# One attention and top-1-expert kernel: expert tables read five halves after their loads, one transposed tile to a half, late expert tiles from half 13 on

## The chip, the cores and the metric

The kernel runs on one NeuronCore of one Trainium2 chip. The metric is the device time of one execution in microseconds (us). Five engines work from instruction streams of their own: TensorE (PE in the profile, with its weight loads as PEld), VectorE (DVE), ScalarE (ACT), GpSimd (POOL) and SyncE (SP), which here only issues transfers. POOL also issues transfers, among them all that add while they copy and all that are indexed.

## The reference, cut to what matters

```python
xn = layernorm(x)                                  # x: 4 batches x 2048 tokens x 512
# attention, 16 heads of 32; q and k go through rfft * sigmoid(mask) * irfft
q, k, v = split(xn @ w_qkv)
attn = softmax(filter(q) @ filter(k).T / sqrt(32))
a = (attn @ v) @ w_out + b_out
# top-1 experts, 8 of them, the first 100 tokens of each, one shared weight matrix
probs = softmax(xn @ w_gate);  best = argmax(probs);  gate = max(probs)
location = cumsum(one_hot(best)) - 1               # over all tokens, in order
kept = location < 100                              # at most 800 tokens in all
f[token] = gate * (xn[token] @ w_expert + b_expert)  if kept else 0
out = x + a + f
```

All arithmetic is in float32.

## The kernel before, in words

**Rounds, blocks and halves.** A round k handles one batch and one group of four heads; there are 16 rounds (k = 4 * batch + group). A round has four blocks of 512 queries, and a block runs over 16 tiles of 128 keys. The work for one key tile is called a half, so that a round has 64 halves (`GH`), a block 16 (`HB`), and the whole kernel 1024. Two halves make a window. In each half PE does four matmuls of queries of a later block against keys, whose row maxima DVE takes, four score matmuls, ACT takes two exponentials, and PE multiplies the tile of the half before with the values (four matmuls into one bank, called the products here), which DVE adds to `num`.

**The side work.** All else is done beside this: projections of the next round, one 128-token piece to a step (16 small matmuls and a copy by ACT); the closing steps of the block before (`fold`, eight `invert`, `divide`, four `result`, then `add`, which adds a 1 MB chunk `y` to the output by a POOL transfer); the transposing of the next batch's normalized tokens (`turn`, four transposes and a copy); the routing of tokens to experts; and the experts themselves. `at(half, step)` appends a step to the agenda of a half, and `behind` puts it after all others of that half. `level` then spreads the projection pieces over the halves by a release, a latest half, and the costs that the other steps have declared.

**The denominators.** After each window POOL issues a 1 MB transfer that adds the tile `odd` into the tile `even` (`pair`, in the next window), and a window later adds the running sum to it with two instructions of its own (`add_to`). There are three buffers for `odd` and five for `even`. An exponential into `odd` therefore waits for the landing of the pair transfer of three windows before.

**The experts.** Routing writes each kept token's number and gate into one of four DRAM tables by indexed transfers. In round 12, the first of the last batch, `place_experts` lays out what follows: `begin` loads the expert weights, the bias and the four tables, reduces the tables on DVE (`entry`, `who`) and clears the first token buffer; `clear_rest` clears the second; `fetch` gathers seven tiles of tokens; `measure` takes their statistics on DVE; `scale` makes their factors on POOL (four small instructions); `expert(i)` normalizes tile i on ACT, transposes tile i-1 and multiplies tile i-2, for the first four tiles. Three late tiles are transposed and multiplied in the last round, as `LATE` says: one half for `turn_row`, four for `expert_columns`. Each tile's result is then added to the output rows in three POOL steps, two halves apart: `gather_row` (indexed read of the output), `add_row`, `scatter_row` (indexed write).

**Order.** `InOrder` keeps every instruction of an engine in program order, so an instruction that waits holds all behind it on its engine. All these instructions are recorded through one helper, and the profile has them at line 83; they are told apart by their tiles.

Of the kernel before, what the change touches and what calls it, by code (L numbers as in the profile page):

```python
# [12 lines left out]
F32 = mybir.dt.float32  # L13
# [20 lines left out]
SLOTS = E * CAP  # L34
ST = -(-SLOTS // P)
EARLY = 4
LATE = ((14, 15, 16, 22, 23), (24, 25, 26, 27, 28), (29, 30, 31, 32, 38))
NTAB = 4
FAR = 1 << 20
EPS = 1e-5  # L40
# [62 lines left out]
def attention_and_top1_experts(ctx: ExitStack, tc: tile.TileContext, a: dict, out: bass.AP):  # L103
# [457 lines left out]
    def expert_steps():  # L561


        def begin():
            w_exp = chunk("w_exp")
            on.sync.dma_start(out=w_exp, in_=a["L0_ffn_w_expert"].rearrange("(r p) n -> p r n", p=P))
            b_exp = work.tile([P, DM], F32, tag="b_exp", name="b_exp", bufs=1)
            on.sync.dma_start(out=b_exp, in_=a["L0_ffn_b_expert"].partition_broadcast(P))
            entries = small.tile([P, NTAB, ST, 2], F32, name="entries")
            for i, table in enumerate(tables):  # L570
                on.sync.dma_start(out=entries[:, i], in_=table.rearrange("(t p) c -> p t c", p=P))
            entry = small.tile([P, ST, 2], F32, name="entry1")
            for i, op in enumerate((ALU.min, ALU.max)):
                on.vector.tensor_reduce(
                    entry[:, :, i], entries[:, :, :, i].rearrange("p n t -> p t n"), AX.X, op
                )
            who = small.tile([P, ST], I32, name="who")
            on.vector.tensor_copy(who, entry[:, :, 0])
            xg = [chunk("xg"), small.tile([P, ST - TQ, DM], F32, name="xg1")]
            on.gpsimd.memset(xg[0], 0.0)  # L580
            mv = small.tile([P, ST, 2], F32, name="mv1")
            index = [bass.IndirectOffsetOnAxis(ap=who[:, i : i + 1], axis=0) for i in range(ST)]
            bound = {"bounds_check": B * S - 1, "oob_is_err": False}
            taken.update(mv=mv, w_exp=w_exp, b_exp=b_exp, entry=entry, index=index, bound=bound, xg=xg)

        def clear_rest():
            on.gpsimd.memset(taken["xg"][1], 0.0)

        def row(i):
            return taken["xg"][i // TQ][:, i % TQ, :]  # L590

        def fetch(i):
            on.gpsimd.indirect_dma_start(row(i), None, rows, taken["index"][i], **taken["bound"])

        def measure(i):
            stats = small.tile([P, 6], F32, name="stats1")
# [12 lines left out]
        def turn_row(i):  # L609
            px = bank()  # L610
            for r in range(NR):
                on.tensor.transpose(px[:, r * P : (r + 1) * P], row(i)[:, r * P : (r + 1) * P], ident)
            taken["xt"] = work.tile([P, QB], F32, tag="byx", name="xt", bufs=1)
            on.scalar.copy(taken["xt"], px)

        def expert_columns(i, q):
            cols = slice(q * P, (q + 1) * P)
            pe = bank()[:, cols]
            for r in range(NR):
                columns(  # L620
                    pe,
                    taken["xt"][:, r * P : (r + 1) * P],
                    taken["w_exp"][:, r, cols],
                    start=(r == 0),
                    stop=(r == NR - 1),
                )
            on.vector.tensor_tensor(row(i)[:, cols], pe, taken["b_exp"][:, cols], ALU.add)
            if q == NR - 1:
                on.scalar.activation(row(i), row(i), AF.Copy, scale=taken["entry"][:, i : i + 1, 1])

        def expert(i):

            if 2 <= i < EARLY + 2:
                at = slice(i - 2, i - 1)
                pe = bank()
                for r in range(NR):
                    on.tensor.matmul(
                        pe,
                        lhsT=taken["xt"][:, r * P : (r + 1) * P],
                        rhs=taken["w_exp"][:, r, :],  # L640
                        start=(r == 0),
                        stop=(r == NR - 1),
                    )
# [11 lines left out]
        return clear_rest, begin, fetch, measure, scale, expert, turn_row, expert_columns  # L655

    def gather_row(i):
        if i < EARLY:
# [366 lines left out]
    def place_experts(start):  # L1025


        clear_rest, begin, fetch, measure, scale, expert, turn_row, expert_columns = expert_steps()
        first = start + 36
        at(first, begin)  # L1030
        at(first + 5, clear_rest)
        for i in range(ST):
            at(first + 2 + 2 * i, fetch, i)
            at(start + (46, 47, 48, 53, 55, 56, 57)[i], measure, i)
        at(first + 22, scale)
        for i in range(ST):
            at(first + 26 + 2 * i, expert, i, cost=(NR if 2 <= i < EARLY + 2 else 0) + (1 if 1 <= i <= EARLY else 0))
        tail = start + 3 * GH
        for i, (turned, *places) in enumerate(LATE):
            at(tail + turned, turn_row, EARLY + i, cost=0.5)  # L1040
            for q, half in enumerate(places):
                at(tail + half, expert_columns, EARLY + i, q, cost=1)
        for i in range(ST):
            free = start + GH + i * HB + 26 if i < EARLY else tail + (25, 30, 39)[i - EARLY]
            for step in (gather_row, add_row, scatter_row):
                at(free, step, i)
                free += 2
# [64 lines left out]
        for n in range(NQ):  # L1112
            at(start + GH - 10 + n * TQ, key_steps, n)

    TURNS = (2, 4, 6, 6, 6, 7, 7, 8, 12, 12, 12, 13, 16, 19, 21, 22)
    SPENT = GH - HB - MAX_AHEAD // 2 + TQ
    ROUTE = len(first_route)
    assert ROUTE == 12 + NT + 1
# [174 lines left out]
```

## Time and profile before

| what | value |
|---|---|
| median of 3 runs | 4135.46 us (4131.81 to 4139.23) |
| the profiled execution | 4130.4 us, of which the span is 4128.6 us |
| granted TensorE clock | 0.999 of full speed |
| PE busy | 4105.5 us (99% of the span) |
| DVE busy | 3418.3 us (83%) |
| POOL busy | 3015.6 us (73%) |
| ACT busy | 2486.1 us (60%) |
| POOL's transfer queue | 601.63 MB, 74.7% of 16 engines' span |

The page gives busy time for each engine, the span in 40 slices, the transfer queues, and the chain of work that ended last. The timeline lists instructions with start, duration and, in square brackets, the idle time of the engine ahead of it and what ended that. Since a half has one group of products (PE `odd,v` or `even,v`), the distance from the start of one such group to the next is the length of a half, and what PE does in between says which side work it held.

### The profile page before, as it was taken

To read this page: it belongs to the slowest core of one execution; us is meant where nothing else is said; L and a number is where in the kernel's file an instruction comes from. 1 tells how busy PE (TensorE), PEld (TensorE's weight loads), DVE (VectorE), ACT (ScalarE), POOL (GpSimd) and SP (SyncE) were. 2 spreads that over 40 slices of the span, in tenths; PEclk is the share of its full clock that TensorE was granted. 3 is DMA by queue.
4 is the path that set the end of the run, shared out by engine and by line. 5 is a ranking of instruction groups with operands and counts; after the bars stand their busy time and mean duration, and the time that the engine had idled before them with its cause. 6 is when DMAs were issued, how large, how long until landed. Compare 5 with 4: busy or idle time off the path is not lost.

```text
span 4128.6 us, 122052 instructions
## 1 busy us (share of the span) xinstructions
PE 4105.5 (99%) x53184; PEld 1832.0 (44%) x53184; DVE 3418.3 (83%) x4876; ACT 2486.1 (60%) x3424; POOL 3015.6 (73%) x2122
## 2 busy tenths in 40 slices
PE   9999999999999999999999999999999999999999
PEld 5444445444444444444444444444444444444442
DVE  7888887978888888797888888888788888888885
ACT  4555565676655556567665556566666555665665
POOL 1678776776887777676787766767678777786787
PEclk9999999999999999999999999999999999999999
DMA  4787887987788878899788788789887887877877
GB/s 127 147 165 154 160 165 160 226 186 147 154 161 162 163 155 161 188 203 193 145 158 160 158 161 160 159 191 208 171 160 151 173 163 150 170 163 156 163 152 147
DMA packets 179488, 680.81 MB, mean 165 GB/s; under 512 B 23478, under 2 KB 54360, under 8 KB 114184
## 3 DMA queue, kind: packets, MB, share of 16 engines
q0 software_dynamic: 109856, 601.63, 74.7%
q1 hardware_dynamic: 69024, 71.34, 5.3%
q8 instruction: 416, 6.82, 0.6%
q14 instruction: 120, 0.98, 0.1%
q10 hardware_dynamic: 72, 0.03, 0.0%
HBM read 71.07 MB, written 87.91 MB: 39 GB/s over the span
## 4 chain that ended last, share of the span: by engine, by line
PE 97%; DVE 1%; DMA 1%; POOL 0%; issue 0%; ACT 0%; SPq 0%; POOLq 0%; ACTq 0%; DVEq 0%
PE array L83 97%; DVE part L83 1%; POOL even L83 0%; DMA even<-odd 0%; DMA entries<-table 0%; DMA odd<-in_L_attn_w_qkv_dram 0%; ACT xs L83 0%; DVE num L83 0%; ACT xnT L83 0%; DVE factor L83 0%; DMA table<-entry,slot 0%; DVE stats L83 0%; POOL out_dram L83 0%; ACT odd L83 0%; POOL rest L83 0%
## 5 line engine op out<-in xcount | busy, mean ns | idle before, releaser
L83 DVE TENSOR_REDUCE part<-array 128x1 f32<-128x512 f32 (+1 forms) x3066 | 2480.7, 865 | 630.4 <-PE array L83 625.4
L83 POOL TENSOR_TENSOR even<-even 128x1024 f32<-128x1024 f32 x876 | 2123.9, 2527 | 466.7 <-DMA even<-odd 465.8
L83 PE MATMUL array<-keys,q 32*128 32x512 f32 x8192 | 2040.9, 613 | 2.5 <-ACT keys L83 0.8
L83 PE MATMUL array<-q,steps_of_keys 32*128 32x512 f32 x8128 | 2009.7, 614 | 0.2
L83 ACT ACTIVATE odd<-array 128x1024 f32<-128x1024 f32 x1024 | 994.7, 1021 | 462.5 <-PE array L83 388.0
L83 ACT ACTIVATE even<-array 128x1024 f32<-128x1024 f32 x1014 | 983.7, 1021 | 417.8 <-PE array L83 409.5
L83 PEld LDWEIGHTS array<-keys,q 32*128 32x128 f32 x8192 | 760.1, 184 | 540.7 <-DVE part L83 326.7
L83 PEld LDWEIGHTS array<-q,steps_of_keys 32*128 32x128 f32 x8128 | 690.4, 183 | 243.4 <-issue 227.0
L83 DVE TENSOR_TENSOR num<-num,array 128x512 f32<-128x512 f32 x960 | 651.0, 678 | 37.7 <-PE array L83 37.7
L83 POOL DMA_DIRECT2D even<-odd x504 | 462.4, 917 | 277.1 <-ACT odd L83 235.6
L83 PEld LDWEIGHTS array<-xnT,w 128*32 128x32 f32 x16384 | 460.0, 110 | 286.3 <-DVE part L83 196.0
L83 PE MATMUL array<-odd,v 128*32 128x512 f32 x4096 | 546.3, 605 | 0.5 <-DVE part L83 0.5
L83 PE MATMUL array<-even,v 128*32 128x512 f32 x4056 | 540.1, 605 | 3.3 <-DVE part L83 3.3
L83 PE MATMUL array<-xnT,w 128*32 128x128 f32 x16384 | 534.7, 273 | 1.1 <-ACT xnT L83 1.0
L83 PEld LDWEIGHTS array<-w,xnT 128*32 128x32 f32 x8192 | 231.5, 110 | 144.6 <-DVE part L83 100.3
L83 DVE RECIPROCAL factor<-den 128x64 f32<-128x64 f32 x504 | 274.7, 546 | 0.0
L83 PE MATMUL array<-w,xnT 128*32 128x128 f32 x8192 | 267.9, 273 | 0.1
L83 PE MATMUL array<-wo,ot 128*32 128x512 f32 x2048 | 266.7, 593 | 0.0
L83 PEld LDWEIGHTS array<-odd,v 128*32 128x32 f32 x4096 | 80.7, 108 | 388.6 <-DVE part L83 380.6
L83 PEld LDWEIGHTS array<-even,v 128*32 128x32 f32 x4056 | 79.8, 108 | 387.9 <-DVE part L83 383.4
L83 POOL DMA_DIRECT2D out_dram<-y x63 | 87.4, 1387 | 156.3 <-ACT y L83 112.1
L83 ACT COPY keys<-array 128x128 f32<-128x128 f32 x256 | 68.2, 266 | 176.8 <-PE array L83 172.3
(152 smaller groups left out, 1540.5 us busy)
## 6 DMA issues: line engine op xcount, KB each, us to landing
even<-odd POOLq DMA_DIRECT2D x504, 1024.0 KB, 8.3
out_dram<-y POOLq DMA_DIRECT2D x63, 1024.0 KB, 9.9
xs<-in_L_attn_x_dram SPq DMA_DIRECT2D x96, 256.0 KB
out_dram<-in_L_attn_x_dram SPq DMA_DIRECT2D x16, 1024.0 KB
w<-wd SPq DMA_DIRECT2D x30, 256.0 KB
w<-in_L_attn_w_qkv_dram SPq DMA_DIRECT2D x16, 256.0 KB
wo<-in_L_attn_w_out_dram SPq DMA_DIRECT2D x16, 256.0 KB
negm<-row SPq DMA_DIRECT2D x192, 4.0 KB
```

Source lines behind the costliest of these rows:

```text
L83: done = act(*args, **kwargs)
```

## The change

The tables are now read by DVE in a step of its own, `read_tables`, five halves after `begin` issued their loads; `begin` keeps the loads and the clearing of the first buffer, and the clearing of the rest moves from five halves after `begin` to two. The gathers of tokens start at half 42 of round 12 rather than 38, the statistics are spread to halves 46, 48, 53, 55, 57, 59 and 61, `scale` moves from half 58 to 62, and the expert steps move by one half. `LATE` starts the late tiles at half 13 of the last round without holes, and the three POOL steps of these tiles start at halves 24, 28 and 33 rather than 25, 30 and 39. `TURNS`, the halves in which the 16 tiles of the next batch are transposed, no longer names a half twice. The halves that `level` finds for projections move with these costs.

```diff
-LATE = ((14, 15, 16, 22, 23), (24, 25, 26, 27, 28), (29, 30, 31, 32, 38))
+LATE = ((13, 14, 15, 16, 22), (22, 23, 24, 25, 26), (27, 28, 29, 30, 31))
...
             for i, table in enumerate(tables):
                 on.sync.dma_start(out=entries[:, i], in_=table.rearrange("(t p) c -> p t c", p=P))
+            xg = [chunk("xg"), small.tile([P, ST - TQ, DM], F32, name="xg1")]
+            on.gpsimd.memset(xg[0], 0.0)
+            mv = small.tile([P, ST, 2], F32, name="mv1")
+            taken.update(mv=mv, w_exp=w_exp, b_exp=b_exp, entries=entries, xg=xg)
+
+        def read_tables():
+            entries = taken["entries"]
             entry = small.tile([P, ST, 2], F32, name="entry1")
             for i, op in enumerate((ALU.min, ALU.max)):
                 on.vector.tensor_reduce(
...
             who = small.tile([P, ST], I32, name="who")
             on.vector.tensor_copy(who, entry[:, :, 0])
-            xg = [chunk("xg"), small.tile([P, ST - TQ, DM], F32, name="xg1")]
-            on.gpsimd.memset(xg[0], 0.0)
-            mv = small.tile([P, ST, 2], F32, name="mv1")
...
         first = start + 36
         at(first, begin)
-        at(first + 5, clear_rest)
+        at(first + 2, clear_rest)
+        at(first + 5, read_tables)
         for i in range(ST):
-            at(first + 2 + 2 * i, fetch, i)
-            at(start + (46, 47, 48, 53, 55, 56, 57)[i], measure, i)
-        at(first + 22, scale)
+            at(first + 6 + 3 * i // 2, fetch, i)
+            at(start + (46, 48, 53, 55, 57, 59, 61)[i], measure, i)
+        at(first + 26, scale)
         for i in range(ST):
-            at(first + 26 + 2 * i, expert, i, cost=(NR if 2 <= i < EARLY + 2 else 0) + (1 if 1 <= i <= EARLY else 0))
+            at(first + 27 + 2 * i, expert, i, cost=(NR if 2 <= i < EARLY + 2 else 0) + (1 if 1 <= i <= EARLY else 0))
...
-            free = start + GH + i * HB + 26 if i < EARLY else tail + (25, 30, 39)[i - EARLY]
+            free = start + GH + i * HB + 26 if i < EARLY else tail + (24, 28, 33)[i - EARLY]
             for step in (gather_row, add_row, scatter_row):
                 at(free, step, i)
                 free += 2
...
-    TURNS = (2, 4, 6, 6, 6, 7, 7, 8, 12, 12, 12, 13, 16, 19, 21, 22)
+    TURNS = (2, 4, 6, 7, 8, 9, 10, 12, 13, 14, 15, 16, 18, 20, 21, 22)
```

More of the change, by code (lines that the diff above doesn't have):

```diff
@@ L578, in begin @@
             on.vector.tensor_copy(who, entry[:, :, 0])
-            xg = [chunk("xg"), small.tile([P, ST - TQ, DM], F32, name="xg1")]
-            on.gpsimd.memset(xg[0], 0.0)
-            mv = small.tile([P, ST, 2], F32, name="mv1")
             index = [bass.IndirectOffsetOnAxis(ap=who[:, i : i + 1], axis=0) for i in range(ST)]
             bound = {"bounds_check": B * S - 1, "oob_is_err": False}
-            taken.update(mv=mv, w_exp=w_exp, b_exp=b_exp, entry=entry, index=index, bound=bound, xg=xg)
+            taken.update(entry=entry, index=index, bound=bound)
         def clear_rest():
@@ L653, in expert @@
                 )
-        return clear_rest, begin, fetch, measure, scale, expert, turn_row, expert_columns
+        return begin, clear_rest, read_tables, fetch, measure, scale, expert, turn_row, expert_columns
     def gather_row(i):
@@ L1025, in place_experts @@
     def place_experts(start):
-        clear_rest, begin, fetch, measure, scale, expert, turn_row, expert_columns = expert_steps()
+        begin, clear_rest, read_tables, fetch, measure, scale, expert, turn_row, expert_columns = expert_steps()
         first = start + 36
         at(first, begin)
-        at(first + 5, clear_rest)
+        at(first + 2, clear_rest)
+        at(first + 5, read_tables)
         for i in range(ST):
-            at(first + 2 + 2 * i, fetch, i)
-            at(start + (46, 47, 48, 53, 55, 56, 57)[i], measure, i)
-        at(first + 22, scale)
+            at(first + 6 + 3 * i // 2, fetch, i)
+            at(start + (46, 48, 53, 55, 57, 59, 61)[i], measure, i)
+        at(first + 26, scale)
         for i in range(ST):
-            at(first + 26 + 2 * i, expert, i, cost=(NR if 2 <= i < EARLY + 2 else 0) + (1 if 1 <= i <= EARLY else 0))
+            at(first + 27 + 2 * i, expert, i, cost=(NR if 2 <= i < EARLY + 2 else 0) + (1 if 1 <= i <= EARLY else 0))
         tail = start + 3 * GH
```

## The prediction

> **What bounds the kernel now.** I read the page first. Its chain of what ended last is nearly all PE:
>
> ```profile
> span 4128.6 us, 122052 instructions
> PE 4105.5 (99%) x53184; PEld 1832.0 (44%) x53184; DVE 3418.3 (83%) x4876; ACT 2486.1 (60%) x3424; POOL 3015.6 (73%) x2122
> ...
> PE 97%; DVE 1%; DMA 1%; POOL 0%; issue 0%; ACT 0%; SPq 0%; POOLq 0%; ACTq 0%; DVEq 0%
> ```
>
> PE's work stays the same, so only what a half costs beside its PE work can change. Next I read the timeline for the lengths of halves (start of one products group to the next). They repeat to 0.01 us for the same side work. PE rows of round 3, halves 6 to 10, score and maxima rows left out:
>
> ```profile
> 872.14 1.07 PE L83 MATMUL array<-odd,v 128*32 128x512 f32 x8
> 873.14 1.82 PE L83 MATMUL array<-square,xs 128*128 128x128 f32 x12
> ...
> 877.45 1.07 PE L83 MATMUL array<-even,v 128*32 128x512 f32 x8
> 878.44 1.09 PE L83 MATMUL array<-square,xs 128*128 128x128 f32 x8
> ...
> 882.02 1.07 PE L83 MATMUL array<-odd,v 128*32 128x512 f32 x8
> 882.90 1.06 PE L83 MATMUL array<-xnT,w 128*32 128x128 f32 x32
> 883.89 0.66 PE L83 MATMUL array<-square,xs 128*128 128x128 f32 x4
> ...
> 886.40 1.07 PE L83 MATMUL array<-even,v 128*32 128x512 f32 x8
> 887.29 1.06 PE L83 MATMUL array<-xnT,w 128*32 128x128 f32 x32
> ...
> 890.20 1.06 PE L83 MATMUL array<-odd,v 128*32 128x512 f32 x8
> ```
>
> Three turns (xs x12): 5.31 us; two turns: 4.57; one projection and one turn: 4.38; one projection: 3.80. By the same reading all over the trace: two projections 4.67, a `result` or `fold` alone 3.78, with a projection 4.66, with a turn 4.55. Then the chain in order of time and the waits, for the places where PE is not the last. In round 12, half 36, DVE waits for the tables:
>
> ```profile
> 3262.90 7.88 DMA entries<-table
> ...
> 3270.97 0.31 DVE L83 TENSOR_REDUCE entry<-entries 128x7 f32<-128x28 f32 x2 [3.19 <-DMA entries<-table]
> ...
> 3272.03 1.07 PE L83 MATMUL array<-even,v 128*32 128x512 f32 x8 [3.06 <-DVE part L83]
> ```
>
> And at the end POOL and its transfers, not PE, set the pace:
>
> ```profile
> 4028.86 1.31 POOL L83 DMA_DIRECT2D out_dram<-y  x1 [1.59 <-ACT y L83]
> ...
> 4040.78 1.10 POOL L83 DMA_INDIRECT w<-out_dram,who  x1 [1.58 <-DMA out_dram<-y]
> ...
> 4060.39 0.90 POOL L83 DMA_DIRECT2D even<-odd  x1
> ...
> 4070.04 1.94 ACT L83 ACTIVATE odd<-array 128x1024 f32<-128x1024 f32 x2 [4.27 <-DMA even<-odd]
> ```
>
> The first two show POOL held until the y add has landed, 11.7 us after its issue; the last two that an exponential waits 4.27 us for a pair transfer issued late.
>
> **The change part by part.** *Turns.* No PE work is added. In rounds 3, 7 and 11 the halves 6, 7, 9, 10, 12, 14, 15, 18, 19 and 20 sum to 5.31 + 4.57 + 3.80 + 3.80 + 5.22 + 3.80 + 3.92 + 3.78 + 4.55 + 3.78 = 42.53 us. In the changed program's order seven of them hold a projection and a turn, two a result and a turn, one a result: 6 x 4.38 + 4.50 + 2 x 4.55 + 3.78 = 43.66. That is +1.1 a round, +3.4 for three. In return three projections a round come out of later halves: in rounds 6 and 10 halves 14, 15, 16 drop from two projections to one (-0.87 each), 20 and 21 lose theirs beside a result and a fold (-0.88 each), and 10 and 12 gain one (+0.87 each): -2.63, twice, -5.3. Loads of token tiles move on SP, but each keeps four halves, 15 us, ahead of its use, more than the two of before.
>
> *Tables.* Half 36 falls from 7.09 to 3.78: -3.3. The three DVE rows of 0.47 us in all go to half 41, where DVE has 0.32 us free (idle before its maxima in such halves): +0.15. What was covered by the stall comes 3.3 us earlier, POOL's pair transfers among them; from half 37 to 57 those land 7 us or more ahead of the exponential that needs them, so nothing new waits there. The seven gathers are the same in number; the first stands at half 42 and its tile is measured at 46, 15 us later, for 4 us of landing.
>
> *Statistics.* In halves with an `invert` a measure costs 0.3 us (3.80 to 4.12). Before there were three such, now four, at 55, 57, 59, 61: +0.35.
>
> *Projections and experts in rounds 13 and 14.* The expert halves move by one and pair differently with results: +0.7; half 44 of round 14 loses a second projection: -0.9. In round 15 halves 13 and 14 go from 3.80 + 4.65 to 3.65 + 3.80: -1.0. What follows half 21 there is counted below.
>
> Sum so far: 3.4 - 5.3 - 3.15 + 0.35 - 0.2 - 1.0 = -5.9 us.
>
> *A wait on ACT that is new.* `scale` moves to half 62, and ACT's `expert(0)` to 63: one half between them instead of four. On POOL `scale` now stands behind the pair transfer and the adds of window 31. In the trace `scale` ran 9 us late:
>
> ```profile
> 3362.09 0.26 POOL L83 TENSOR_SCALAR rstd<-mv 128x7 f32<-128x7 f32 x1
> ...
> 3373.01 1.57 POOL L83 TENSOR_TENSOR ot<-num,factor 128x512 f32<-128x512 f32 x1
> 3374.24 1.19 POOL L83 DMA_DIRECT2D even<-odd  x1
> 3374.85 5.28 POOL L83 TENSOR_TENSOR even<-even 128x1024 f32<-128x1024 f32 x2
> ```
>
> Its four instructions take 2.5 us. If POOL is as late as here, less those 2.5, `scale` ends near 3380, while ACT would start `expert(0)` at 3373.9: ACT is held 6 us, and with it the copy that frees a bank and the next exponentials, so PE stops for as long, 6.5 us with the 0.8 us normalize. But in the trace POOL at 3341 and 3351 waited for the landing of three transfers behind each other, and their issue follows from `fetch` and the clearing, which now take less of POOL ahead of half 42. Adding up POOL's rows from half 36 in the new order (two gathers of 1.1 us fewer ahead of half 42, two more behind it, where transfers were awaited anyway) I get the pair of half 54 1.6 us earlier against PE, and `scale` at its end 3.9 us after ACT is ready: PE loses 3.4. I take 3.4; the ends are 0 (POOL not late) and 6.5.
>
> *Waits on POOL at the end.* In round 15 the order is now scatter(4) then gather(5) with nothing between, scatter(5) then gather(6), and the y add of half 37 then scatter(6). Each second one waits for the landing of the first, and POOL holds all behind it. A scatter lands 2.8 us after its start (median), 1.7 after its own 1.1: twice +1.9 with the restart. POOL is without a gap from 4000 to 4027, so these and the gather and add of tile 6, which now precede the y add (1.1 + 1.3), move the y add from 4028.9 to 4033.2. It lands 6 us after the pair transfer ahead of it, at about 4046; before, POOL spent 2.7 + 1.6 + 1.9 us waiting in this stretch, now some 11. The pair transfer after it moves from 4030.9 to 4048, and behind that, at 6 to 8 us a window, the one at 4060.4 to about 4069. It lands some 7 us later than 4069.9, and the exponential at 4070.0 waits that much longer. All that PE gains or loses between half 21 and there is swallowed by this wait. +7; the ends are 3 (scatter lands at once, y in the 9.4 us median) and 12.4, as told below. If the scatter cost nothing it would be 0.
>
> [...] The row says 11.7, with two other 1 MB transfers about, and I go by the row.
>
> Sum: -5.9 + 3.4 + 7 = **+4.5 us** on the profiled execution's 4130.4 (span 4128.6 and 1.8 around it), so 4134.9. That execution was 5.1 under the median of the three runs; on the median it is **4140.0**.
>
> **The rivals.** *Slower.* The mechanism is scatter(6) behind the y add, round 15 half 37. The last 1 MB read of the output starts when that scatter has landed (4061.3 before); it now starts near 4050, in the midst of the pair transfers that POOL waits for. A 1 MB transfer takes 5.4 us of the queue (74.7% of 4128.6 over the 569 issued), so the term could be 12.4 and the sum +9.9: 4145.4. It decides from a tail of 10.8 on. For it: the last of three transfers in a row landed 16.7 us after its issue, at 3351.8. Against it: that read stood in the way at 4061 before as well. *Waits that hide.* POOL catches up in the four halves that now hold less, ACT waits for nothing, and the tail costs 3: -2.9, 4132.6; with no tail at all 4129.6. Against it: POOL had no gap from 4000 to 4027. *The tables still wait.* Loads landing 13 us later would bring the 3.3 us back: 4143.3. Against it: the last landed at 3270.8, 7.9 us after its start, and the new reads stand 13 us behind that.
>
> **How the numbers follow.** About 0.2% (8.3 us) is what a measurement of this kernel can tell from no change. My forecast, both waits near the middle, has 0.50, and its own range is 4134 to 4146; the slower rival 0.27; the hidden waits 0.15; the tables 0.02; a wait that I don't see, slower, 0.06. Faster by 0.2% needs no wait and 2.4 us more than my gains: 0.07, out of the hidden waits. Slower: 0.27 + 0.06 + 0.03 from the edge of the forecast = 0.36. Same: 0.57. Range 4130 (no tail) to 4151 (12.4 and 6.5 together, plus 2 of the 3.7 us by which the runs lie off their median).
>
> **What would show it.** Half 36 of round 12 at 3.8 us; in rounds 3, 7, 11 no half above 4.6 by turns; ACT `xg<-xg,shift,rstd` with idle time ended by POOL; POOL `out_dram<-xg,who` with some 11 us ended by DMA `out_dram<-y`; the exponential into `odd` of half 49 waiting longer than 4.27. I am wrong if POOL runs ahead there, or if DVE stalls in halves that now hold a turn and an invert.

## The result, and the profile after

Over 13 runs each the changed kernel takes 4145.31 us in the median (4143.35 to 4147.67) and the kernel before 4138.09 us (4131.81 to 4140.25). The ratio is 1.0022, with a 95% interval of 1.0014 to 1.0029: some 6 to 12 us slower, an interval that holds the 0.2% (8.3 us) below which the prediction calls a change the same. The prediction was 4140.0 us, which is 4.5 us over the three runs of before that it started from; over all 13 the kernel before is 2.6 us slower than over those three, and the changed kernel 7.2 us slower than it.

The page of the changed kernel has PE as busy as before, and nothing but PE in the chain that ended last:

```profile
span 4143.5 us, 122062 instructions
...
PE 4115.2 (99%) x53184; PEld 1836.1 (44%) x53184; DVE 3419.3 (83%) x4879; ACT 2487.8 (60%) x3424; POOL 3016.4 (73%) x2122
...
PE 97%; DVE 1%; POOL 0%; DMA 0%; issue 0%; ACT 0%; ACTq 0%; POOLq 0%; DVEq 0%
```

PE has the same 53184 matmuls and is 9.7 us busier, so that somewhere it is slower at the same work. Some half of that are the stray halves named at the end of this section; the low clock shown before them, which the prediction did not have, is another part.

The turns are as they were foreseen. In the timeline of the changed kernel, PE rows of round 3 (start, duration, engine, operation and tiles; score and maxima rows left out), halves 6 to 9 hold one projection and one turn each and are 4.38 us long, where 5.31, 4.57, 4.38 and 3.80 stood before:

```profile
872.24 1.06 PE L83 MATMUL array<-odd,v 128*32 128x512 f32 x8
873.12 1.06 PE L83 MATMUL array<-xnT,w 128*32 128x128 f32 x32
874.11 0.66 PE L83 MATMUL array<-square,xs 128*128 128x128 f32 x4
...
876.62 1.06 PE L83 MATMUL array<-even,v 128*32 128x512 f32 x8
...
881.00 1.06 PE L83 MATMUL array<-odd,v 128*32 128x512 f32 x8
...
885.39 1.07 PE L83 MATMUL array<-even,v 128*32 128x512 f32 x8
```

The wait for the tables in half 36 of round 12 is gone (7.09 to 3.96 us), but half 41, in which they are now read, has grown from 3.80 to 4.75. The timeline of the changed kernel, DVE rows of that half and the products that follow:

```profile
3290.18 0.23 DVE L83 TENSOR_REDUCE entry<-entries 128x7 f32<-128x28 f32 x2
3290.34 1.32 DVE L83 CAST who<-entry 128x7 int32<-128x7 f32 x1
3291.58 2.41 DVE L83 TENSOR_REDUCE part<-array 128x1 f32<-128x512 f32 x3
...
3292.31 1.06 PE L83 MATMUL array<-odd,v 128*32 128x512 f32 x8 [0.88 <-DVE part L83]
```

The conversion of 128 x 7 token numbers (`who`) takes 1.32 us; before it took 0.17. PE waits 0.88 us for the maxima behind it.

The two waits that were foreseen on POOL are both there. At the end of round 12 the timeline, POOL and ACT rows, has `shift` ready at 3379.97 and ACT idle for 3.02 us before it:

```profile
3377.80 1.52 POOL L83 TENSOR_TENSOR rstd<-rstd,power 128x7 f32<-128x7 f32 x1
3379.39 0.21 POOL L83 TENSOR_TENSOR shift<-mv,rstd 128x7 f32<-128x7 f32 x1
3379.69 0.28 POOL L83 TENSOR_SCALAR shift<-shift 128x7 f32<-128x7 f32 x1
...
3380.01 0.81 ACT L83 ACTIVATE xg<-xg,shift,rstd 128x512 f32<-128x512 f32 x1 [3.02 <-POOL shift L83]
```

And in the last round, halves 37 to 43, POOL and ACT rows:

```profile
4040.16 1.27 POOL L83 DMA_DIRECT2D even<-odd  x1
4040.73 2.04 POOL L83 DMA_DIRECT2D out_dram<-y  x1
4055.20 1.09 POOL L83 DMA_INDIRECT out_dram<-xg,who  x1 [12.43 <-PE array L83]
4056.31 0.73 POOL L83 TENSOR_TENSOR xnT<-keys 64x256 f32<-64x256 f32 x1
4056.98 0.91 POOL L83 DMA_DIRECT2D even<-odd  x1
...
4062.58 1.94 ACT L83 ACTIVATE even<-array 128x1024 f32<-128x1024 f32 x2 [9.54 <-POOL even L83]
```

The scatter behind the y add holds POOL for 12.43 us. The row names PE as what ended it; the expert columns that this scatter stores were ready long before, and the experiment that moves the scatter away removes the wait, so it is the landing of the y add. In a second profile of this kernel, in which that landing is recorded, the y add lands at 4053.08 and the scatter starts at 4053.92. Nothing else runs on POOL meanwhile, the running sum of the denominators among it, and so the exponential into `even` of half 42 waits 9.54 us. Half 42 is 11.32 us long instead of 2.29.

The stretches of the same place (length, busy time of PE, PEld, DVE, ACT and POOL with instruction counts, granted clock, DMA share, GB/s) show a second loss behind the wait:

```profile
4055.00:4057.00 2.00, 1.32 (x11) 0.16 (x8) 1.97 (x5) 0.00 (x0) 1.78 (x3) 1.00 0.05 16
4057.00:4060.00 3.00, 0.00 (x0) 0.00 (x0) 1.25 (x3) 0.00 (x0) 3.00 (x4) 0.80 0.69 142
4060.00:4063.00 3.00, 0.00 (x0) 0.00 (x0) 0.00 (x0) 0.42 (x1) 3.00 (x4) 0.50 1.04 213
4063.00:4066.00 3.00, 2.34 (x8) 1.01 (x8) 0.00 (x0) 1.69 (x3) 2.89 (x3) 0.50 0.65 128
4066.00:4069.00 3.00, 3.00 (x16) 0.65 (x14) 0.42 (x1) 1.81 (x3) 3.00 (x3) 0.50 0.90 183
```

While PE stands, its clock falls to 0.50 (from 4058.78 to 4069.02), and stays there for the first 5.4 us in which it works again: the eight products take 1.94 us instead of 1.07.

Two profiles, one of each kernel, differ by 14.9 us in span, which is more than the kernels do. Between 4 and 5 us of that lie in stray halves, 0.35 to 0.6 us longer each, in rounds 1, 4, 12, 13 and 14, in places that the change does not touch; the experiments below show that they are not the change's.

### The profile page after: what moved, and what is told of

It reads as the page before. It is cut to its first block, busy times and chain, and to the rows that moved or that the text cites. A ratio compares the mean times of both kernels' runs of the same rounds, so it can differ in the third digit from the quotient of the medians.

```text
span 4143.5 us, 122062 instructions
## 1 busy us (share of the span) xinstructions
PE 4115.2 (99%) x53184; PEld 1836.1 (44%) x53184; DVE 3419.3 (83%) x4879; ACT 2487.8 (60%) x3424; POOL 3016.4 (73%) x2122
## 4 chain that ended last, share of the span: by engine, by line
PE 97%; DVE 1%; POOL 0%; DMA 0%; issue 0%; ACT 0%; ACTq 0%; POOLq 0%; DVEq 0%
PE array L83 97%; DVE part L83 1%; POOL even L83 0%; DMA even<-odd 0%; DVE num L83 0%; DMA freq<-in_c_freq_dram 0%; ACT xs L83 0%; DVE factor L83 0%; ACT xnT L83 0%; POOL xnT L83 0%; DVE stats L83 0%; DVE who L83 0%; POOL ot L83 0%; ACT odd L83 0%; POOL rest L83 0%
## 5 line engine op out<-in xcount | busy, mean ns | idle before, releaser
L83 ACT COPY q<-array 128x128 f32<-128x128 f32 x256 | 67.9, 265 | 184.1 <-PE array L83 184.1
```

The costliest lines, as they stand in the source:

```text
L83: done = act(*args, **kwargs)
```

## The experiments

Medians are compared with runs of the kernel before on the same chip, 29 to 33 of them for the first two groups of four and 21 for the third. The medians of before differ by some 6 us between chips (4131.73 to 4138.09), so that differences to before and ratios are given, and lengths of halves are compared with the first profile of before. The two kernels that measure a price by itself (holds of PE, conversions) ran once each, for their profile, and no time of theirs is compared.

**The kernel before once more.**

> The kernel before, unchanged. Its profiled execution so far took 4130.4 us, while the median of 13 is 4138.1. If that execution was merely at the low end, a second profile shows a span near 4136 with the extra 6 to 8 us spread over halves that did not change (stray halves longer by 0.3 to 0.6 us), and of the 14.9 us between the two profiles only some 7 belong to the change. If the extra 0.3 to 0.6 us halves of the profile after come from the change itself, the second profile of before repeats the first to within 2 us, half by half.

Median 4131.63 against 4131.97 us, ratio 0.9999 (0.9990 to 1.0008); the profile has a span of 4130.6 us and repeats the first half by half, except halves 32, 36 and 37 of round 12 (4.67 to 5.07, 7.09 to 6.52, 3.78 to 5.23) and a trade of 0.41 us between halves 49 and 50 of round 15. The stray halves of the first profile after are not in it, and not in the second profile after either, but the kernel with the tables alone, below, has 3.75 us of them in rounds 4 and 8. They seem to go with the chip: halves 14 and 16 of round 4 are 0.2 to 0.6 us longer in the first profile after and in all four profiles of the third group, whose chip is also some 5 us slower for the kernel before (4136.74 against 4131.97 and 4131.73), and in none of the eight profiles of the first two groups. Half 37 is of interest: the wait in half 36 was shorter by 0.57 us and the half behind it longer by 1.45, with a granted clock of 0.50 from 3272.2 to 3275.6. A wait of PE can have a second part, and the tables' wait cost before 3.1 us (first profile) or 4.0 (this one: 11.75 - 7.74 for both halves).

**POOL's starts as before.**

```diff
-            free = start + GH + i * HB + 26 if i < EARLY else tail + (24, 28, 33)[i - EARLY]
+            free = start + GH + i * HB + 26 if i < EARLY else tail + (25, 30, 39)[i - EARLY]
```

> The changed kernel with the three POOL starts of the late tiles as before (25, 30, 39). If the scatter directly behind the y add is what costs PE its stall in round 15 (POOL idle 12.43 us, the exponential of half 42 waiting 9.54 us), the stall of 9 us goes, a part of it (about 1 to 3 us, the waits before had at halves 49 to 50) comes back later, and the kernel takes 4145.3 - 7.5 = 4137.8 us (4136 to 4140), which is level with before. If the tail is slow because of the late tiles' new halves or because POOL is late anyway, it stays at 4143 or more and the wait of the exponential only moves.

4.0 us over before, ratio 1.0009 (1.0000 to 1.0018), at the edge of no change. The stall of half 42 is gone: from half 37 on this kernel is within 0.5 us of before, while the changed one lost 7.5 us there. No exponential waits over the 4.3 us of before. That the late tiles' new halves cost the tail, the rival, falls. But its median is not level with before, as it should have been with a wait of 2.5 us in round 12. In this profile that wait cost PE 6.25 us (halves 63 and 0), and the stretches around it say why:

```profile
3375.40:3377.30 1.90, 0.00 (x0) 0.00 (x0) 0.43 (x1) 0.99 (x3) 1.74 (x4) 0.89 0.15 44
3377.30:3379.30 2.00, 1.98 (x6) 0.51 (x6) 0.00 (x0) 0.90 (x1) 2.00 (x3) 0.50 0.32 66
...
3381.00:3383.00 2.00, 2.00 (x40) 1.47 (x32) 0.69 (x1) 0.00 (x0) 2.00 (x1) 0.50 0.99 201
```

After 1.96 us without a matmul the clock was 0.50 for 6.8 us. In the first profile of the changed kernel PE stood 1.38 us at this place, the clock stayed at 1.00, and the loss was 2.65.

**The third start alone as before.**

```diff
-            free = start + GH + i * HB + 26 if i < EARLY else tail + (24, 28, 33)[i - EARLY]
+            free = start + GH + i * HB + 26 if i < EARLY else tail + (24, 28, 39)[i - EARLY]
```

> The changed kernel with only the third POOL start as before (24, 28, 39), so that gather(5) still stands directly behind scatter(4), but scatter(5) and the y add have no indexed transfer directly behind them. If the scatter behind the y add is nearly the whole cost, this takes the same as with all three starts back, within 1 us (4137 to 4140), with one POOL wait of 2.5 us ahead of the second gather left in the trace and no exponential waiting for it. If the gathers behind scatters share the cost, 4140 to 4143.

7.6 us over before, ratio 1.0018 (1.0009 to 1.0027): 3.6 more than with all three back. The scatter behind the y add is not the whole cost; my guess that it was nearly all is refuted. With the gather of tile 5 still directly behind the scatter of tile 4, POOL comes late to the y add, which now stands between two pair transfers issued within 2.1 us:

```profile
4032.97 1.17 POOL L83 DMA_DIRECT2D even<-odd  x1
4033.55 1.93 POOL L83 DMA_DIRECT2D out_dram<-y  x1
4034.34 1.88 POOL L83 TENSOR_TENSOR xnT<-keys 64x256 f32<-64x256 f32 x1
4035.01 2.06 POOL L83 DMA_DIRECT2D even<-odd  x1
4041.57 4.68 POOL L83 TENSOR_TENSOR even<-even 128x1024 f32<-128x1024 f32 x2 [4.50 <-DMA even<-odd]
4046.93 1.09 POOL L83 DMA_INDIRECT w<-out_dram,who  x1 [0.68 <-DMA out_dram<-y]
```

The gather behind it starts 13.4 us after the issue of the y add, against 11.9 before. An exponential into `even` then waits 3.17 us at 4064.5, and the clock is 0.50 from 4065.9 to 4079.6. Tile 4's steps stand one half earlier here than in the kernel above and tile 5's two, so that the gather behind the scatter is the likely cause of the 3.6 us, but was not tried by itself.

**Statistics and scale as before.**

```diff
-            at(start + (46, 48, 53, 55, 57, 59, 61)[i], measure, i)
-        at(first + 26, scale)
+            at(start + (46, 47, 48, 53, 55, 56, 57)[i], measure, i)
+        at(first + 22, scale)
```

> The changed kernel with the statistics at halves 46, 47, 48, 53, 55, 56, 57 and scale at 58, as before, the experts still from 63 on. If ACT's wait for POOL's scale costs PE its 2.5 us in half 63 of round 12 (6.41 against 3.91), that half falls to 3.9 to 4.0, one half with an invert fewer pays for a statistic, and the time is 4145.3 - 2.5 - 0.3 = 4142.5 us (4141.5 to 4143.5). If the time that PE gains there is only given back at the next pair transfer, half 63 falls and the time stays at 4145.

3.4 us over before, ratio 1.0009 (0.9999 to 1.0018). Half 63 is 3.91 us and ACT's `xg<-xg,shift,rstd` waits for nothing. The tail of the changed kernel is unaltered in it (half 42 is 11.23 us). The gain is more than the 2.8 that I expected, but its size is not well known, since the changed kernel did not run on this chip: it was 7.2 over before at first, which makes 3.8 us, and is 11.1 over before on the next chip, below, which makes 7.7.

**The changed kernel once more.**

> The changed kernel, unchanged, beside the kernels it is compared with. Its median so far is 7.2 us over before. Two things are to be seen in a second profile. First, the conversion of the token numbers in round 12, half 41, which took 0.17 us before: if DVE is held by the POOL instruction running beside it, it takes anything from 0.2 to 2.35 us and ends with a POOL instruction's end; if it has merely become slower there, it takes 1.3 us again. Second, the stall of half 63: with the granted clock staying at 1.00 it costs 2.5 us, with the clock falling to 0.50 it costs 6, while the wait itself stays at 3 to 3.6 us.

11.1 us over before, ratio 1.0028 (1.0017 to 1.0040). ACT waits 5.93 us for `shift` this time, and half 63 with the half after it costs 8.18 us:

```profile
3378.04 0.81 ACT L83 ACTIVATE xg<-xg,shift,rstd 128x512 f32<-128x512 f32 x1 [5.93 <-POOL shift L83]
```

The expected span of 3 to 3.6 us was too narrow. In the first profile PE lost 1.8 us in half 43 and 0.4 in three halves of the round before this place, time in which POOL can catch up; this was not tried by itself. The conversion takes 1.25 us here, and 1.90, 2.21 and 0.92 in the three kernels above: not one value, and each ends 26 to 28 ns after a POOL add does.

**Both waits removed.** The two diffs above together (POOL's starts, statistics and scale).

> The changed kernel with both of its new waits removed: the POOL starts (25, 30, 39) and statistics and scale as before. If the two waits are all that the change costs, the gains remain (2.7 us by the per-half sums up to round 15, half 14) and the tail is that of before: 2 to 4 us under before, ratio 0.9990 to 0.9995. If removing one wait lets another take its place (POOL's pace sets the end of round 12 whatever scale does), it is level with before or above it, 0 to +4 us.

4.5 us under before, ratio 0.9989 (0.9980 to 0.9999). With ranges that do not overlap (4124.7 to 4129.4 against 4141.2 to 4144.3), the two waits are what the change costs, and what remains of it is a gain of about the size that the prediction had without them. Between this kernel and the changed one lie 15.6 us on one chip.

**The scatter behind the y add, in the kernel before.**

```diff
-            free = start + GH + i * HB + 26 if i < EARLY else tail + (25, 30, 39)[i - EARLY]
+            free = start + GH + i * HB + 26 if i < EARLY else tail + (25, 33, 39)[i - EARLY]
```

> The kernel before with one number changed: the second late tile's POOL steps start at 33 rather than 30, so that its scatter stands at half 37, directly behind the y add, and nothing else moves (gather(6) stays at 39, now behind that scatter). If a scatter directly behind the y add is by itself the mechanism, POOL idles 10 to 13 us before it, the exponential of half 42 waits some 9 us, and the kernel takes 8 us more than before (6 to 10). If it needs the other changes of the tail (late tiles, gathers behind scatters), 0 to 3 us.

7.3 us over before, ratio 1.0017 (1.0008 to 1.0026), as expected; one number is enough. The shape differs. POOL idles 11.96 us, and the exponentials wait three times, 4.22, 2.15 and 3.20 us, rather than once:

```profile
4030.62 1.29 POOL L83 DMA_DIRECT2D out_dram<-y  x1 [1.31 <-ACT y L83]
4043.87 1.07 POOL L83 DMA_INDIRECT out_dram<-xg,who  x1 [11.96 <-PE array L83]
...
4051.32 1.94 ACT L83 ACTIVATE even<-array 128x1024 f32<-128x1024 f32 x2 [4.22 <-POOL even L83]
```

The clock is at 0.50 from 4054.8 to 4058.2 and again from 4068.4 to 4082.1. A part of the difference of the two profiles is not the scatter's: the clock fell in half 37 of round 12 here, which cost 1.6 us.

**An improved version.** Both waits removed (statistics and scale by the diff above), the conversion on ACT, and the late tiles' rows added to the output ahead of the y add:

```diff
-            on.vector.tensor_copy(who, entry[:, :, 0])
+            on.scalar.copy(who, entry[:, :, 0])
...
-            free = start + GH + i * HB + 26 if i < EARLY else tail + (24, 28, 33)[i - EARLY]
+            free = start + GH + i * HB + 26 if i < EARLY else tail + (23, 27, 31)[i - EARLY]
             for step in (gather_row, add_row, scatter_row):
                 at(free, step, i)
-                free += 2
+                free += 2 if i < EARLY or step is gather_row else 0
```

> Both waits removed as in the kernel before this one but one, and two more things: the conversion of the token numbers on ACT instead of DVE, and the late tiles' steps ahead of the y add: gathers at halves 23, 27 and 31 of the last round, each add and its scatter two halves later, so that no indexed transfer stands behind the y add. [...] If the gather behind the y add cost before its 4.27 us wait and the low clock after it, the tail gets 2 to 5 us shorter. In sum 5 to 9 us under before; if the pair transfers behind the y add are late by themselves, the tail stays and it is 3 to 4 us under before.

5.7 us under before, ratio 0.9987 (0.9978 to 0.9996): it beats both kernels, by the low end of what I expected, but not clearly the kernel with both waits removed, which is 1.3 us slower with a range that overlaps. The one line of the turns, below, does as much on another chip. The conversion takes 0.20 us on ACT, and half 41 is 4.26 us rather than 4.67, still 0.46 over the 3.80 of before: ACT idles for 1.46 us until DVE's reductions are done, and the conversion stands ahead of a copy of keys, which starts 2.88 us into the half rather than 2.01. The expected sum of 5 to 9 us counts on half 41 as well, for which these 0.41 us are what the run shows. The tail is hardly shorter: from half 37 to the end it gained 0.7 us against before rather than 2 to 5. The pair transfers behind the y add are late by themselves (POOL waits 4.55 and 4.62 us for the next two), and two exponentials now wait for POOL's sum, 2.33 us at 4050.8 and 1.94 us at 4057.0.

**The price of a wait on PE, and the clock.** In the kernel before, ACT is held at 24 places in quiet halves of 3.8 us by copies of a dead tile:

```diff
+    def hold_act(n):
+        for _ in range(n):
+            on.scalar.copy(freq[:, 1, :], freq[:, 0, :])
+
+    for k in (1, 5, 9):
+        for half, n in zip((6, 13, 24, 29, 40, 45, 55, 61), (9, 11, 13, 15, 18, 21, 24, 28)):
+            at(k * GH + half, hold_act, n)
```

> The kernel before with 24 holds of known length: in rounds 1, 5 and 9, at halves 6, 13, 24, 29, 40, 45, 55 and 61, ACT copies a small dead tile 9, 11, 13, 15, 18, 21, 24 or 28 times, so that PE waits for ACT from under 1 us up to some 6 us, in halves of 3.8 us whose length is otherwise known to 0.01 us. Nothing is left out. If the falling clock is what made the same wait cost 2.5 us in one execution and 6 in others, the loss of each hold is PE's idle time alone where the clock stays at 1.00, and 1.5 to 3 us more where it falls to 0.50, in this and the next half; the fall comes never below 1 us of idle time, sometimes between 1.5 and 3.5 and always above some length. If the extra loss is the queues behind the wait (POOL's transfers), the clock stays at 1.00 with these short holds and the loss equals the idle time.

| copies | longest stretch without a matmul, us | lost in this and the next half, us, rounds 1, 5, 9 | clock fell |
|---|---|---|---|
| 9 | 0.50 | 1.63, 1.63, 1.63 | no, no, no |
| 11 | 1.15 | 2.28, 3.92, 3.91 | no, yes, yes |
| 13 | 1.76 | 3.32, 4.52, 2.89 | no, yes, no |
| 15 | 2.42 | 6.45, 5.18, 6.67 | yes, yes, yes |
| 18 | 3.42 | 7.16, 6.79, 7.22 | yes, yes, yes |
| 21 | 4.41 | 8.14, 7.95, 8.18 | yes, yes, yes |
| 24 | 5.45 | 9.41, 9.31, 9.47 | yes, yes, yes |
| 28 | 6.73 | 10.91, 10.86, 10.94 | yes, yes, yes |

Where the clock stays, a hold costs the longest gap and 1.13 us more, although around the gap of 1.15 us in round 1 PE is busy for all of the 4.20 us ahead (395.00 to 399.20) and the 3 us behind; 3.32 has 0.42 more, at a full clock. Where the clock falls, it costs 1.6 to 3.1 us more than that (3.92 - 2.28; 10.94 - 7.86). The same hold of 1.15 us in round 1 and in round 5, the gap itself and the 3 us after it, round 1 first:

```profile
399.20:400.40 1.20, 0.05 (x4) 0.04 (x3) 0.46 (x1) 1.14 (x5) 1.03 (x2) 1.00 1.05 218
400.40:403.40 3.00, 3.00 (x50) 1.44 (x50) 1.82 (x2) 1.85 (x2) 2.99 (x4) 1.00 0.36 80
...
1463.30:1464.50 1.20, 0.08 (x3) 0.08 (x3) 0.42 (x1) 1.14 (x5) 0.96 (x2) 1.00 0.53 156
1464.50:1467.50 3.00, 3.00 (x14) 0.69 (x18) 1.12 (x1) 1.81 (x2) 2.82 (x2) 0.52 1.07 218
```

PE is busy for all of the 3 us either way, but does 50 matmuls in the one and 14 in the other. The clock fell after none of three gaps of 0.50 us, three of six between 1.15 and 1.76, and all fifteen from 2.42 on. This is the second part of the wait in round 12 and of the tail. The rival, that the queues behind the wait make the loss, falls: with these holds the clock falls, and where it does not, the loss is the same 1.13 us over the gap but for one hold.

The length of the gap is not all that decides. In the first profile of the kernel before, PE waits 3.06 us in half 36 of round 12, longer than any gap of the table that left the clock up, and the clock stays at 1.00 (stretches of that profile, as above):

```profile
3269.00:3271.00 2.00, 0.00 (x0) 0.00 (x0) 0.03 (x1) 1.08 (x2) 2.00 (x2) 1.00 1.00 197
3271.00:3273.00 2.00, 0.97 (x12) 0.40 (x16) 2.00 (x6) 0.00 (x0) 0.34 (x1) 1.00 1.04 201
```

The falls lie on a grid. In the kernel with the holds the clock falls at 467.92, 519.12 and 546.43 us, and the second and third lie 15 and 23 steps of 3.413 us after the first; the other 15 falls at the holds, to the last at 2751.5, lie a whole number of such steps from it too. It stayed low for one, two or three steps (3.41, 6.83 or 10.24 us), in the last round of two kernels above for four (13.65 us). So it is around the first hold of 2.42 us, with the step ahead of the fall, the two low ones and the one behind them:

```profile
464.51:467.92 3.41, 1.67 (x10) 0.37 (x2) 1.80 (x4) 3.09 (x11) 2.63 (x4) 1.00 0.68 156
467.92:474.75 6.83, 6.15 (x50) 2.80 (x54) 1.91 (x2) 2.81 (x6) 5.20 (x3) 0.50 0.68 137
474.75:478.16 3.41, 3.41 (x60) 1.54 (x56) 2.56 (x4) 1.94 (x2) 0.14 (x1) 1.00 0.00 0
```

What decides is not shown: in the 3.41 us ahead of the fall at 1464.62 PE was busy for 2.26 us, and in the first profile of before for 1.74 us in the step from 3267.23 to 3270.64, a whole number of steps (236) ahead of that profile's fall at 4072.78, which left the clock up.

**The price of a conversion.** In the kernel before, 18 conversions in round 5 and 18 reductions of the same size in round 9:

```diff
+    few_i = const.tile([P, 7], I32, name="few_i")
...
+    def convert():
+        on.vector.tensor_copy(few_i, power.rearrange("p (b a) -> p b a", a=2)[:, 0:7, 0])
+
+    def smaller():
+        on.vector.tensor_reduce(few_i.bitcast(F32), power[:, 0:14].rearrange("p (b a) -> p b a", a=2), AX.X, ALU.min)
+
+    for half in range(6, 60, 3):
+        at(5 * GH + half, convert)
+        at(9 * GH + half, smaller)
```

> The kernel before with a price measured by itself: 18 conversions of 128 x 7 numbers from float32 to int32 on DVE in round 5 (the kind that took 0.17 us before and 0.9 to 2.2 us after the change), and 18 reductions of the same size in round 9. Nothing is left out. If DVE's conversion is held by the POOL instruction running beside it, the conversions that start beside a POOL tensor instruction take from 0.2 to 2.35 us and end where it ends, the others 0.17 us, and the reductions take some 0.2 us wherever they stand. If such conversions are just slow in some places (POOL's transfers, the memory), their ends do not fall together with POOL's, and the reductions vary too.

First the profile's summary for that tile (count, then the shortest, the median and the longest in ns), then, from the timeline, POOL and DVE rows of one conversion beside POOL's two adds:

```profile
L83 DVE CAST few_i<-power x18: 107/782/5804, 1382.1 to 1598.9; 128x7 int32<-128x7 f32 x18
L83 DVE TENSOR_REDUCE few_i<-power x18: 109/114/163, 2420.1 to 2617.5; 128x7 f32<-128x14 f32 x18
```

```profile
1403.78 4.98 POOL L83 TENSOR_TENSOR even<-even 128x1024 f32<-128x1024 f32 x2
...
1405.44 3.36 DVE L83 CAST few_i<-power 128x7 int32<-128x7 f32 x1
```

Eleven of the 18 conversions took 0.39 to 5.80 us, and each of the eleven ended 28 to 39 ns after a POOL tensor instruction did (here 1408.76 and 1408.80); the other seven, with no such instruction beside them, took 0.11 to 0.17 us. No reduction took over 0.163 us, though many ran beside the same adds (the one at 2443.11, inside two adds of 5.02 us together, took 0.11). The bound of 2.35 us, one POOL instruction, that I had put on it is wrong: the conversion above began in the first of two adds that follow without a gap and ended with the second, and the longest, 5.80 us, outlasts two such adds (4.98 us).

**The tables alone.** The kernel before, with the three DVE instructions in a step of their own, two halves behind the loads rather than five as in the change:

```diff
+        def read_tables():
...
         at(first, begin)
         at(first + 5, clear_rest)
+        at(first + 2, read_tables)
```

> The kernel before with the reading of the tables alone moved, two halves behind the issue of their loads instead of none (the gathers, statistics and everything else stay). The wait of DVE in half 36 of round 12 cost PE 3.1 to 3.3 us where the clock stayed up, and 4.7 where it fell in half 37. Half 36 falls to 3.8 to 4.0, half 38 pays 0 to 2 us for the conversion beside POOL: the kernel gains 1.5 to 4.5 us, ratio 0.9989 to 0.9997. If the stall is only handed on to POOL's transfers, nothing is gained (1.0000).

2.1 us under before, ratio 0.9996 (0.9987 to 1.0005): within the expected 1.5 to 4.5, but not told from no change. Half 36 is 3.96 us, and halves 38 and 41 are as before. The conversion takes 0.17 us at 3280.07, and POOL's next add starts at 3280.30, so that none stands beside it. The 3.1 us are not handed on inside round 12.

**The turns alone.**

```diff
-    TURNS = (2, 4, 6, 6, 6, 7, 7, 8, 12, 12, 12, 13, 16, 19, 21, 22)
+    TURNS = (2, 4, *range(6, 11), *range(12, 17), 18, 20, 21, 22)
```

> The kernel before with the turns alone spread, one to a half. By the per-half sums of the profile after, rounds 3, 7 and 11 cost 1.27 us more each and rounds 6 and 10 give back 2.62 each: 3 x 1.27 - 2 x 2.62 = -1.4 us, ratio 0.9995 to 1.0000, below what can be told from no change; the halves of rounds 3, 6, 7, 10 and 11 repeat those of the changed kernel to 0.1 us. If the shifted loads of token tiles cost something that the changed kernel hid, it is slower than that by 1 us or more.

6.6 us under before, ratio 0.9984 (0.9975 to 0.9993), not the 1.4 that I expected. The halves of rounds 3, 6, 7, 10 and 11 do repeat those of the changed kernel. The rest lies where I had not looked: `level` places other pieces elsewhere too, half 44 of round 14 loses 0.87 us, halves 14 and 24 of round 15 lose 1.01 each, and the tables' wait in half 36 is 1.77 us shorter in this execution. These make 6.1, and half 31 of round 12 takes 0.7 back. The 1.77 is one profile's, and that wait varies without the change too, so that 3.6 of the 6.6 us are placed for certain. That the shifted loads cost something, the rival, falls.

## Why the prediction was right or wrong

The forecast of a small loss, made of some 6 us of gains and two waits on POOL that outweigh them, is what the runs show; the kernel with both waits removed is 4.5 us under before and the changed one 7 to 11 over. Its sum, +4.5 on the profiled execution, was too low by 3 to 7 us; added to the 13 runs of before rather than to the three, it gives 4142.6 us, 2.7 under the measured 4145.3. Term by term, by lengths of halves against the first profile of before, the first and the second profile after:

| term of the sum | predicted | first | second |
|---|---|---|---|
| turns, rounds 3, 7, 11 | +3.4 | +3.8 | +3.8 |
| projections, rounds 6 and 10 | -5.3 | -5.2 | -5.2 |
| tables, half 36 | -3.3 | -3.1 | -3.1 |
| tables, half 41 | +0.15 | +0.95 | +0.88 |
| statistics | +0.35 | 0 | 0 |
| experts in round 13, half 44 of round 14 | -0.2 | 0 | 0 |
| round 15, halves 13 and 14 | -1.0 | -1.0 | -1.0 |
| ACT's wait for `scale` | +3.4 | +2.65 | +8.2 |
| the tail, from half 37 | +7 | +7.5 | +8.0 |
| the tail, from half 21 | +7 | +8.6 | +8.2 |

*Turns and projections.* Right to 0.4 us in sum: lengths of halves read off for each kind of side work carry over. That the same numbers also move pieces in rounds 14 and 15 was in the sum, but under other headings; it takes the kernel with the turns alone to see that they belong to the turns.

*Statistics and experts.* Both small terms came to nothing: half 59, which got a measure, held 4.00 us already and grows by 0.11 only, and the later experts cost 0.9 in round 13, not 0.7, as much as half 44 of round 14 gives back.

*Tables.* Half 36 is right. The step that failed is "the three DVE rows of 0.47 us in all go to half 41 ... +0.15": one of them took 0.17 us because it stood at 3271.2, where POOL was issuing a transfer and ran no add, and 0.9 to 2.2 us beside POOL's adds. A duration was carried to a place with another neighbour. With the conversion on ACT the half is 0.4 us shorter, in one profile each, and still 0.46 longer than before.

*ACT's wait.* The place and the cause are right, and the size is the term that was mis-sized. I took 3.4 out of 0 to 6.5; it was 2.65 to 8.2 in four executions (6.3 and 6.0 in the kernels with the POOL starts back), and taking it away gave 3.8 or 7.7 us, by the two comparisons of medians. The upper bound fell because it held the time that POOL is late and nothing for PE's clock afterwards: in the second profile after, ACT waits 5.93 us, within the bound, the clock is 0.50 for 6.8 us, and the loss is 8.2.

*The tail.* The order on POOL came out as worked out: the y add 4.4 us later against half 37 (predicted 4.3), POOL standing for 12.4 us where "some 11" was said, and 7 to 8 us lost for 7. The kernel before with that one number changed loses 7.3. What is wrong is the place: the wait was to lengthen the one of 4.27 us at half 49, an exponential into `odd` that needs a pair transfer. POOL's sum into `even` is held first, and an exponential into `even` waits at half 42; half 49 gets shorter by 3.2. The two gathers behind scatters, "twice +1.9", waited 2.56 and 2.02 us, and the kernel with only the third start back, 3.6 us slower than with all three, shows that the first two starts count too. That what PE gains or loses between halves 21 and 37 is swallowed by the tail's wait is not what the rows show: the changed kernel loses 0.3 us there in the second profile (1.2 in the first, most of it stray halves), on top of the tail. The lower bound reads "the 9.4 us median" for a y add's landing; over the whole trace of before it is 9.9.

*The rivals.* The slower one had the right mechanism, the scatter behind the y add, with a y add that lands late among the pair transfers: POOL stood until 14.5 us after its issue, against 11.9 before. Its price for the tail, 12.4, was not reached, nor the 10.8 from which it was to decide. That the time came near its 4145.4 is luck: the other wait, and the 2.6 us by which before is slower over 13 runs than over three, make up for it. The waits did not hide, and the tables did not go on waiting.

*What is open.* Half 31 of round 12 is 0.4 to 1.0 us longer in every kernel with the new turns, and in none without them; PE stands there for up to 0.40 us and the profile names nothing that it waits for; nothing was tried. Why POOL is 3 us less late for `scale` in one execution of the changed kernel than in another was only argued.

## What to carry to other kernels

On an engine that works strictly in order and also issues transfers, leave a window of other work between a long transfer and anything that depends on its landing; one index moved by three halves costs 7 us here. Price a stall on PE as its length and 1.1 us more, and where the clock falls, as it did in three of six holds of 1.15 to 1.76 us and in all from 2.42 us on, with 1.6 to 3.1 us on top. Do not carry the 0.17 us of a short DVE conversion to a place where POOL is adding: beside the adds it took up to 5.80 us. A plan that places work by declared costs moves pieces far from the edit, so try the parts alone: here one line, the turns, is 6.6 us under before on its own, and the whole change without its two waits 4.5.

## What the runs showed of the hardware

*The clock after a stall.* In the first profile of before the granted clock is 1.00 from 10.93 to 4072.78 us, with PE busy for 99% of the span. After a gap in PE's matmuls it fell to 0.50: in the kernel with the holds after none of the three gaps of 0.50 us, three of the six of 1.15 to 1.76 us, and all fifteen from 2.42 us on, at a cost of 1.6 to 3.1 us; in the first profile of before a gap of 3.06 us left it up. The 18 falls at the holds lie whole numbers of steps of 3.413 us apart, and the clock came back after one to three such steps (3.41, 6.83 or 10.24 us), in the last round of two other kernels after four (13.65 us). After the same gap of 1.15 us it fell in rounds 5 and 9 and not in round 1, and in the 3.41 us ahead of the fall at 1464.62 PE was busy for 2.26 us. What decides was not shown.

*DVE's conversion and POOL.* A conversion from float32 to int32 of 128 x 7 numbers took 0.11 to 0.17 us with no POOL tensor instruction beside it (seven of 18). The other eleven took 0.39 to 5.80 us, and each ended 28 to 39 ns after a POOL tensor instruction did, which can be the second in a row (3.36 us, beside two adds of 4.98 us together). A reduction of the same size took 0.109 to 0.163 us, beside such adds as well. Why the one is held and the other is not was not shown.
